# Softmax denominators from 32x32 transposes and one product, one more buffer for high parts, and a different order on VectorE and GpSimd in the second of two attention layers

## Chip, cores and metric

One core of one Trainium2 chip. The metric is the device time of one execution in microseconds (us), lower is better. Engines: TensorE (PE, with its weight loads shown apart as PEld), VectorE (DVE), ScalarE (ACT), GpSimd (POOL), and SyncE (SP), which only issues DMAs. SBUF is the on-chip memory, PSUM the small memory that TensorE writes to.

## The reference

Two self-attention layers over 4 images of 64x64 = 4096 tokens with 256 channels, float32:

```
# layer 0: q, k of width 32, v of width 256
q, k, v = x @ Wq + bq, x @ Wk + bk, x @ Wv + bv
x = gamma * softmax(q @ k.T) @ v + x
# layer 1: f (keys), g (queries) of width 32, v of width 128
f, g, v = x @ Wf + bf, x @ Wg + bg, x @ Wh + bh
x = x + (softmax(g @ f.T) @ v) @ Wo + bo
```

## The kernel before

`fast_path` holds the whole calculation (`general_path` runs only if a range test at the end finds values too large or too small; it did not run here). No maximum is subtracted: the kernel computes `p = exp(score)`, accumulates `p @ v`, and divides by the sum of p at the end.

**Tiling.** A `Step` is one score tile `st` of 128 keys x 1024 (four key tiles by 256 queries in layer 0, two key tiles by 512 queries in layer 1). A block is one set of queries against all keys: 8 steps in layer 0 (16 blocks per image), 16 steps in layer 1 (8 blocks per image). So there are 32 blocks of layer 1 in all. The loop over `steps` (L735) runs image by image, layer 0 then layer 1.

**What a step does.** `scores` (L523) puts the products k*q into PSUM and ScalarE takes `high` (a rounded exp, for split steps) and `p` (L542, L544). `cut_low` (L552) makes `low = p - high` on VectorE, `cut_both` (L557) makes `d` from low and high. TensorE then multiplies high, low and d with three forms of v, each in one pass of float32r. All layer 0 steps are split. In layer 1 only steps 0, 3, 5, 8, 11, 13 (`SPLIT1`) are; the other ten multiply `p` itself in full float32 (two instructions per product). Scores run two steps ahead of the products, and low one step ahead.

**Sums of p in layer 1.** For steps in `MOVED_SUMS` the sum is made by DMAs that GpSimd issues (L548 a copy for the first, L550 adding DMAs for the others) into the tile `p_sum_moved`. For the others VectorE adds into `p_sum` (`add_up`, L564). At the end of a block `end_second` (L654) adds the two (L659), folds 1024 columns to 512 (`sums`, L660), and returns four units, `output(t)`, one for each 128 queries. A unit multiplies the accumulated rows by Wo (L667) and, to get each query's denominator onto its own partition, multiplies the 128x128 block of `sums` by a column of ones (L668). VectorE inverts that column (L670), ScalarE scales the result (L673), GpSimd's queue adds it to `out` in memory by a DMA (L675).

**Order.** `plan` (L702) hands units to steps: the four output units of a block go to steps 1 to 4 of the next block. Projections of coming keys and values (`project_units`: transpose, qk, v) are dealt out in the same way over both layers. The framework traces instructions in program order, then orders each engine's queue itself by a model of readiness, so an engine's queue may differ from the program's order. Tiles with one `tag` share a ring of `bufs` buffers, and a new tile waits until the oldest user is done. The rings here: `t` (high parts, and p of split layer-1 steps) 2, `p` 3, `l` 2, `d` 1 (also p_sum), `e` 1 (p_sum_moved), `small` 4 (residual rows `x_res`, new rows `x1`, outputs `y`), `sums` 1, `qk` 1, `squares` 2; in PSUM `side` 2.

**End.** After the last unit, the range test (L807 to L822) runs over all inverses and decides by a flag whether the general path is needed.

Of the kernel before, what the change touches and what calls it, by code (L numbers as in the profile page):

```python
# [61 lines left out]
S = 32  # L62
# [5 lines left out]
SPLIT1 = (0, 3, 5, 8, 11, 13)  # L68
MOVED_SUMS = (0, 4, 7, 9, 12)

# [168 lines left out]
def fast_path(ctx: ExitStack, tc: tile.TileContext, x, w0, w1, wo, bo, gamma, out, off):  # L239
# [27 lines left out]
    def wide(tag, name, dtype=F32):  # L267
        return work.tile([P, 2 * QB], dtype, tag=tag, bufs={"d": 1, "e": 1, "p": 3}.get(tag, 2), name=name)

# [39 lines left out]
    nc.vector.memset(ones, 1.0)  # L309

    inverse = const.tile([P, 2, B * N // P], F32, name="inverse")
    seen_v = const.tile([P, 2, B * NH], F32, name="seen_v")
# [11 lines left out]
    for l, (q_w, q_b, k_w, k_b, v_w, v_b) in enumerate((w0, w1)):  # L324
        queue = (nc.scalar, nc.gpsimd)[l]
        w_sb = work.tile([P, NCC, 2 * D], F32, tag="small", bufs=4, name=f"wqk_whole{l}")
        b_sb = const.tile([2 * D, 1], F32, name=f"bqk{l}")
        for g, w_dram, b_dram in ((0, q_w, q_b), (D, k_w, k_b)):
            queue.dma_start(w_sb[:, :, g : g + D], w_dram.rearrange("(c p) d -> p c d", p=P))
            queue.dma_start(b_sb[g : g + D, :], b_dram.rearrange("(d o) -> d o", o=1))  # L330
        w_parts = const.tile([P, NCC, 4 * D], F32R, name=f"wqk{l}")
        high, low = w_parts[:, :, : 2 * D], w_parts[:, :, 2 * D :]
        nc.scalar.copy(high, w_sb)
        nc.vector.tensor_sub(low, w_sb, high.bitcast(F32))
        wqk.append(w_parts)
        bqk.append(b_sb)
        v_sb = const.tile([P, NCC, CV[l]], F32, name=f"wv{l}")
        queue.dma_start(v_sb, v_w.rearrange("(c p) d -> p c d", p=P))
        wv.append(v_sb)
# [20 lines left out]
    def bias_units():  # L360


        def issue():
            nc.vector.tensor_scalar(bv, bv, gamma_sb, None, ALU.mult)
            wide_bias = work.tile([P, P], F32, tag="small", bufs=4, name="wide_bias")
            nc.vector.memset(wide_bias, 1.0)
            nc.vector.tensor_scalar(wide_bias, wide_bias, bv1, None, ALU.mult)
            ps = side_psum("ps_bias")[:, :C]
            nc.tensor.matmul(ps, wide_bias, wo_sb, start=True, stop=True)
            nc.vector.tensor_add(bo_sb, bo_sb, ps)  # L370

        return [issue]

    xT, x_parts, k_t, v_t, halves = {}, {}, {}, {}, {}
    qk_dram, x1_dram = {}, {}
    q_t, moved_sums, first_p, waiting = {}, {}, [], {}

# [34 lines left out]
    def project_units(b, l, h):  # L412
# [5 lines left out]
        def qk_unit():  # L418
            ps = side_psum(f"psqk_{b}_{l}_{h}")[:, :QB0]
            for c in range(NCC):  # L420
                for n in range(2):
# [6 lines left out]
                    )  # L428
            whole = data.tile([2 * D, QB0], F32, tag="qk", name=f"qk_{b}_{l}_{h}")
            lead = b == l == 0 and h % 2 == 1  # L430
# [7 lines left out]
            top, bottom = slice(0, 2 * D), slice(2 * D, P)  # L438
            nc.scalar.copy(whole, ps[bottom, :])
            nc.vector.scalar_tensor_tensor(whole, ps[top, :], bqk[l], whole, ALU.add, ALU.add)  # L440
            nc.scalar.copy(parts[top, :], whole)
# [49 lines left out]
    def load_rows(dst, parts, which, order):  # L491
        for n, h in enumerate(order):
            nc.gpsimd.dma_start(dst[n * D : (n + 1) * D, :], parts[h, which])

# [15 lines left out]
    def small(name):  # L510
        return work.tile([P, C], F32, tag="small", bufs=4, name=name)


    class Step:
# [8 lines left out]
        def scores(self):  # L523
            b, l, j, i = self.b, self.l, self.j, self.i
            n = 2 * QB // G[l]
            q0 = j * n % QB
            index = j * NI[1] + i
            tag = "pair" if l == 1 and index > 0 and index % 2 == 0 else "st"
            st = ps_main.tile([P, G[l], n], F32, tag=tag, name=f"st_{self.key}")
            for g in range(G[l]):  # L530
                kt = G[l] * i + g
                nc.tensor.matmul(  # L532
                    st[:, g, :],
                    k_t[b, l, kt // NT][:, kt % NT * P : (kt % NT + 1) * P],
                    q_t[b, l, j * n // QB][:, q0 : q0 + n],
                    start=True,
                    stop=True,
                )
            s_flat = st.rearrange("p g n -> p (g n)")
            if self.split:  # L540
                self.high = wide("t", f"high_{self.key}", F32R)
                nc.scalar.activation(self.high, s_flat, AF.Exp, bias=down)  # L542
            self.p = wide("t" if self.split and l == 1 else "p", f"p_{self.key}")
            nc.scalar.activation(self.p, s_flat, AF.Exp)  # L544
            if l == 1 and i in MOVED_SUMS:
                if i == MOVED_SUMS[0]:
                    moved_sums[b, j] = wide("e", f"p_sum_moved_{b}_{j}")
                    nc.gpsimd.dma_start(moved_sums[b, j], self.p)  # L548
                else:
                    nc.gpsimd.dma_start(moved_sums[b, j], self.p, accum_op=ALU.add)  # L550

        def cut_low(self):  # L552
            if self.split:
                self.low = wide("l", f"low_{self.key}", F32R)
                nc.vector.tensor_sub(self.low, self.p, self.high.bitcast(F32))  # L555

        def cut_both(self):  # L557
            if self.split:
                self.d = wide("d" if self.l == 0 else "l", f"d_{self.key}", F32R)
                nc.vector.scalar_tensor_tensor(  # L560
                    self.d, self.low.bitcast(F32), -UP, self.high.bitcast(F32), ALU.mult, ALU.add
                )

        def add_up(self, p_sum):  # L564
            if self.l == 0 or self.i in MOVED_SUMS:
                return
            kept = [i for i in range(NI[1]) if i not in MOVED_SUMS]
            if self.i == kept[0]:
                first_p.append(self.p)
            elif self.i == kept[1]:  # L570
                nc.vector.tensor_add(p_sum, first_p.pop(0), self.p)
            else:
                nc.vector.tensor_add(p_sum, p_sum, self.p)  # L573

# [78 lines left out]

    def end_second(b, j, acc, p_sum, o):  # L654
        key = f"{b}_{j}"
        for h in range(QB // QB0):
            nc.vector.tensor_add(o[h][:, :QB0], o[h][:, :QB0], acc[1][:, h * QB0 : (h + 1) * QB0])
        sums = work.tile([P, QB], F32, tag="sums", bufs=1, name=f"sums_{key}")
        nc.vector.tensor_add(p_sum, p_sum, moved_sums[b, j])  # L659
        nc.vector.tensor_add(sums, p_sum[:, :QB], p_sum[:, QB:])  # L660

        def output(t):
            def issue():
# [3 lines left out]
                nc.tensor.matmul(ps[:, :C], part, wo_sb, start=True, stop=True)  # L667
                nc.tensor.matmul(ps[:, C : C + 1], sums[:, tok], ones[:, :1], start=True, stop=True)  # L668
                n = (b * N + j * QB) // P + t
                nc.vector.reciprocal(inverse[:, 1, n : n + 1], ps[:, C : C + 1])  # L670

# [6 lines left out]

        return [output(t) for t in range(NT)]

    def run(units):
        for u in units:
            u()


# [9 lines left out]
    steps[1].scores()  # L695
    steps[0].cut_low()
    beyond = Step(B, 1, 0, 0)
    beyond.scores, beyond.split = nothing, False
    keys = [(b, l, j) for b in range(B) for l in range(2) for j in range(NB)][NB:]
    acc, p_sum, units = None, None, {}  # L700

    def plan(b, l, j, ends):  # L702
# [20 lines left out]
        else:  # L723
            for n, u in enumerate(ends):
                put(1 + n, u)
        if b + 1 < B:
            for h in range(NH):
# [7 lines left out]
    for n, s in enumerate(steps):  # L735
        b, l, j = s.b, s.l, s.j
        if s.first:
            units = plan(b, l, j, ends)
            acc = [ps_main.tile([P, QB], F32, tag=f"acc{a}", name=f"acc{a}_{b}_{l}_{j}") for a in range(2)]
            if l == 0:  # L740
                pair = ps_main.tile([P, 2, QB], F32, tag="pair", name=f"acc_pair_{b}_{j}")
                acc += [pair[:, a, :] for a in range(2)]
            if l == 1:
                p_sum = wide("d", f"p_sum_{b}_{j}")
        if l == 0 and s.last:
# [20 lines left out]

        s.cut_both()
        after.cut_low()
        s.add_up(p_sum)
        todo = units.get(s.i, [])  # L770
# [30 lines left out]
        if s.last:  # L801
            ends = end_first(b, j, acc) if l == 0 else end_second(b, j, acc, p_sum, o)
    run(ends)

    good = small("good").rearrange("p (l n) -> p l n", l=2)  # L807
    nc.vector.tensor_scalar(good, inverse, 1.0 / SUM_MAX, None, ALU.is_ge)
    nc.vector.tensor_scalar(inverse, inverse, 1.0 / SUM_MIN, None, ALU.is_le)
    nc.vector.tensor_mul(good, good, inverse)  # L810
    nc.vector.tensor_scalar(seen_v, seen_v, VALUE_MAX, None, ALU.is_le)
    size = const.tile([P, 1], F32, name="size")
    nc.vector.tensor_mul(size, gamma_sb, gamma_sb)
    nc.vector.tensor_scalar(size, size, GAMMA_MAX**2, None, ALU.is_le)
    low = const.tile([P, 1], F32, name="low")
    for seen, axes in ((good, AX.XY), (seen_v, AX.XY)):
        nc.vector.tensor_reduce(low, seen, axes, ALU.min)
        nc.vector.tensor_mul(size, size, low)
    nc.vector.tensor_scalar(low, size, 1.0, None, ALU.is_lt)
# [53 lines left out]
```

## Time and profile before

| | us |
|---|---|
| median of 3 runs | 3158.69 (3158.46 to 3160.62) |
| the profiled execution's own time | 3155.92 |
| its span, first to last instruction | 3154.1 |
| TensorE matmul busy | 3116.3 (99%) |
| TensorE weight loads busy | 2672.0 (85%) |
| VectorE busy | 2689.1 (85%) |
| ScalarE busy | 2140.1 (68%) |
| GpSimd busy | 900.7 (29%) |
| granted TensorE clock | 0.998 of full |

Everything below is read from one profiled execution. Its own time is 2.8 us under the median of the unprofiled runs and 1.8 us over its span. "Busy" of TensorE is modelled: its matmuls are pipelined, so what counts is when the next one starts. A few per cent of matmul records can be missing from a trace.

### The profile page before, as it was taken

What the parts mean: (1) busy time and instruction counts of PE and PEld (TensorE: products, weight loads), DVE (VectorE), ACT (ScalarE), POOL (GpSimd) and SP (SyncE); (2) the same over time, 40 slices, a digit from 0 to 9 for tenths busy, and PEclk for the clock granted to TensorE, in tenths of its full rate; (3) what the DMA queues carried; (4) which work ended last, traced back from release to release, by engine and by line L of the source; (5) the groups of instructions that cost most, each with busy time, mean ns of one, the idle gap of its engine ahead of it and who ended that gap; (6) DMA issues with size and microseconds to landing.
All of it is one profiled execution on the core that took longest, in us unless ns stands there. A gap on an engine that the chain in (4) does not pass through costs nothing.

```text
span 3154.1 us, 54090 instructions
## 1 busy us (share of the span) xinstructions
PE 3116.3 (99%) x19908; PEld 2672.0 (85%) x19908; DVE 2689.1 (85%) x3237; ACT 2140.1 (68%) x2835; POOL 900.7 (29%) x1108
## 2 busy tenths in 40 slices
PE   8999999999999999999999999999999999999997
PEld 7999998666799999866679999976668999996664
DVE  7888888888888888888888888898888888888876
ACT  7666666777666666777766666677776666666674
POOL 5232224222422222422242222232223222233221
PEclk9999999999999999999999999999999999999999
DMA  4121114555512121555541112255554111125454
GB/s 119 43 53 47 48 48 104 107 108 105 104 44 51 41 53 47 113 101 112 107 93 47 49 45 51 51 116 107 105 113 81 48 46 47 49 65 105 97 95 73
DMA packets 391392, 239.49 MB, mean 76 GB/s; under 512 B 266672, under 2 KB 355248, under 8 KB 391120
## 3 DMA queue, kind: packets, MB, share of 16 engines
q0 software_dynamic: 68160, 134.86, 22.0%
q1 hardware_dynamic: 322048, 100.76, 13.4%
q8 instruction: 161, 2.64, 0.4%
q14 instruction: 111, 0.91, 0.1%
q10 hardware_dynamic: 912, 0.33, 0.1%
HBM read 82.58 MB, written 67.11 MB: 47 GB/s over the span
## 4 chain that ended last, share of the span: by engine, by line
PE 91%; DVE 3%; DMA 2%; issue 2%; ACT 1%; POOL 0%; SPq 0%; DVEq 0%; ACTq 0%; POOLq 0%
PE acc L600 24%; PE acc L582 23%; PE acc_pair L582 23%; PE st L532 14%; PE psv L464 4%; PE psqk L422 2%; PE pso L667 2%; DVE d L560 1%; DVE low L555 1%; ACT p L544 1%; DVE p_sum L573 1%; DMA p_sum_moved<-p 0%; DMA squares<-in_x 0%; PE pso L668 0%; DMA squares<-x_dram 0%
## 5 line engine op out<-in xcount | busy, mean ns | idle before, releaser
L542 ACT ACTIVATE high<-st,down 128x1024 fp32r<-128x1024 f32 x704 | 786.5, 1117 | 703.2 <-PE st L532 362.8
L544 ACT ACTIVATE p<-st 128x1024 f32<-128x1024 f32 x1024 | 1042.5, 1021 | 166.3 <-PE st L532 143.8
L560 DVE SCALAR_TENSOR_TENSOR d<-low,high 128x1024 fp32r<-128x1024 f32 x704 | 871.0, 1237 | 227.0 <-PE acc_pair L582 223.7
L555 DVE TENSOR_TENSOR low<-p,high 128x1024 fp32r<-128x1024 f32 x704 | 936.6, 1330 | 142.6 <-ACT p L544 141.6
L532 PE MATMUL st<-q,k 128*128 128x256 f32 (+1 forms) x3072 | 706.3, 338 | 2.5 <-DMA k<-qk_parts 1.4
L600 PE MATMUL acc<-p,v 128*128 128x512 f32 x1280 | 611.0, 597 | 0.0
L532 PEld LDWEIGHTS st<-q,k 128*128 128x128 f32 x3072 | 470.0, 189 | 103.3 <-issue 40.6
L639 POOL TENSOR_TENSOR x_res<-x,bo 128x256 f32<-128x256 f32 x128 | 212.5, 1660 | 879.3 <-DVE x L628 879.2
L600 PEld LDWEIGHTS acc<-p,v 128*128 128x128 f32 x1280 | 233.1, 189 | 161.8 <-issue 143.4
L573 DVE TENSOR_TENSOR p_sum<-p_sum,p 128x1024 f32<-128x1024 f32 x288 | 352.6, 1224 | 9.4 <-ACT p L544 5.8
L582 PE MATMUL acc<-v0h,high 128*128 128x258 f32 x2048 | 341.6, 284 | 1.2 <-ACT high L542 1.2
L582 PE MATMUL acc<-v0d,d 128*128 128x258 f32 x2048 | 339.2, 287 | 2.6 <-DVE d L560 2.2
L582 PE MATMUL acc<-v0l,low 128*128 128x256 f32 (+1 forms) x2048 | 329.3, 283 | 0.6 <-DVE low L555 0.5
L582 PE MATMUL acc_pair<-v0h,high 128*128 128x258 f32 x2048 | 329.8, 283 | 0.0
L582 PE MATMUL acc_pair<-v0l,low 128*128 128x256 f32 (+1 forms) x2048 | 328.8, 282 | 0.0
L582 PE MATMUL acc_pair<-v0d,d 128*128 128x258 f32 x2048 | 328.5, 282 | 0.0
L582 PEld LDWEIGHTS acc<-v0h,high 128*128 128x128 f32 x2048 | 286.0, 189 | 3.1 <-issue 1.4
L582 PEld LDWEIGHTS acc<-v0d,d 128*128 128x128 f32 x2048 | 281.5, 190 | 5.6 <-DVE d L560 4.9
L582 PEld LDWEIGHTS acc<-v0l,low 128*128 128x128 f32 x2048 | 282.2, 190 | 1.8 <-DVE low L555 1.3
L582 PEld LDWEIGHTS acc_pair<-v0h,high 128*128 128x128 f32 x2048 | 282.1, 189 | 0.0
L582 PEld LDWEIGHTS acc_pair<-v0l,low 128*128 128x128 f32 x2048 | 281.1, 189 | 0.0
L582 PEld LDWEIGHTS acc_pair<-v0d,d 128*128 128x128 f32 x2048 | 281.0, 189 | 0.0
(108 smaller groups left out, 3332.5 us busy)
## 6 DMA issues: line engine op xcount, KB each, us to landing
p_sum_moved<-p POOLq DMA_DIRECT2D x160, 512.0 KB, 4.7
x_res<-in_x SPq DMA_DIRECT2D x128, 128.0 KB, 2.1
qk_dram<-qk_parts SPq DMA_DIRECT2D x128, 128.0 KB, 1.9
x_dram<-x SPq DMA_DIRECT2D x128, 128.0 KB, 1.7
out<-x_res SPq DMA_DIRECT2D x128, 128.0 KB, 1.7
squares<-x_dram SPq DMA_DIRECT2D x512, 32.0 KB, 1.9
out<-y POOLq DMA_DIRECT2D x128, 128.0 KB, 3.2
q<-qk_dram POOLq DMA_DIRECT2D x252, 64.0 KB, 2.2
```

The source lines that it names most:

```text
L422: nc.tensor.matmul(ps, wqk[l][:, c, :], x_parts[key][n][:, c, :], start=(c == n == 0), stop=(c == NCC - 1 and n == 1),)
L464: nc.tensor.matmul(ps[:, t, :], xT[key][:, c, t * P : (t + 1) * P], wv[l][:, c, :], start=(c == 0), stop=(c == NCC - 1),)
L532: nc.tensor.matmul(st[:, g, :], k_t[b, l, kt // NT][:, kt % NT * P : (kt % NT + 1) * P], q_t[b, l, j * n // QB][:, q0 : q0 + n], start=Tru ...
L542: nc.scalar.activation(self.high, s_flat, AF.Exp, bias=down)
L544: nc.scalar.activation(self.p, s_flat, AF.Exp)
L555: nc.vector.tensor_sub(self.low, self.p, self.high.bitcast(F32))
L560: nc.vector.scalar_tensor_tensor(self.d, self.low.bitcast(F32), -UP, self.high.bitcast(F32), ALU.mult, ALU.add)
L573: nc.vector.tensor_add(p_sum, p_sum, self.p)
L582: nc.tensor.matmul(acc[2 * s + which][:, :width], p[:, g * QB0 + s * P : g * QB0 + (s + 1) * P], v0[self.i][v][:, g, :width], start=self.f ...
L600: nc.tensor.matmul(acc[which], v_part[:, g, :], p[:, g * QB : (g + 1) * QB], start=first and g == 0, stop=last and g == G[1] - 1,)
L639: nc.gpsimd.tensor_add(x_old[s], x_new[s], bo_sb)
L667: nc.tensor.matmul(ps[:, :C], part, wo_sb, start=True, stop=True)
```

## The change

In the second layer the six moved steps become (3, 4, 6, 7, 9, 12): the base is step 3's own p tile, written by ScalarE into ring `e`, so no copying DMA; five adding DMAs follow. VectorE's adds go from ten to nine in a block. The column of ones is replaced, in 31 of the 32 blocks, by two VectorE instructions (`turn`: a 32x32 block transpose of `sums`, and a sum over groups of 32 columns into `part_sums`, 128x16) and one product with a fixed 0/1 matrix `same` (`denominators`), followed by four inversions of 32 partitions x 4. These two units take steps 1 and 2 of the next block, the four output units steps 3 to 6. The last block keeps the column of ones. `sums` now lives in `p_sum`, in ring `d`, until `turn` has read it. `same` is built by GpSimd at the start with seven small instructions. Ring `t` has three buffers, `small` three, `sums` and `qk` are gone (the qk unit works in PSUM and in `qk_parts`). `issue_after` queues instructions of one engine behind a given one: in layer 1 what VectorE does after the cuts (sums, units) goes behind the latest low or d, and each adding DMA goes behind the last load of q or k traced before it. The range test is divided: all but the last block's inverses are tested in step 13 of the last block, the last four columns at the end.

```diff
-MOVED_SUMS = (0, 4, 7, 9, 12)
+MOVED_SUMS = (3, 4, 6, 7, 9, 12)
...
-        return work.tile([P, 2 * QB], dtype, tag=tag, bufs={"d": 1, "e": 1, "p": 3}.get(tag, 2), name=name)
+        return work.tile([P, 2 * QB], dtype, tag=tag, bufs={"d": 1, "e": 1, "p": 3, "t": 3}.get(tag, 2), name=name)
...
+    same = const.tile([P, P], F32, name="same")
+    nc.gpsimd.tensor_copy(same[:, :S], ident[:, :S])
+    for a in range(1, P // S):
+        nc.gpsimd.tensor_add(same[:, :S], same[:, :S], ident[:, a * S : (a + 1) * S])
+    for a in range(1, P // S):
+        nc.gpsimd.tensor_copy(same[:, a * S : (a + 1) * S], same[:, :S])
...
-            nc.scalar.copy(whole, ps[bottom, :])
-            nc.vector.scalar_tensor_tensor(whole, ps[top, :], bqk[l], whole, ALU.add, ALU.add)
+            whole, rest = ps[top, :], parts[top, :].bitcast(F32)
+            nc.scalar.copy(rest, ps[bottom, :])
+            nc.vector.scalar_tensor_tensor(whole, whole, bqk[l], rest, ALU.add, ALU.add)
...
-            nc.gpsimd.dma_start(dst[n * D : (n + 1) * D, :], parts[h, which])
+            loads[0] = nc.gpsimd.dma_start(dst[n * D : (n + 1) * D, :], parts[h, which])
...
-        return work.tile([P, C], F32, tag="small", bufs=4, name=name)
+        return work.tile([P, C], F32, tag="small", bufs=3, name=name)
...
+            base = l == 1 and i == MOVED_SUMS[0]
+            self.p = wide("e" if base else "t" if self.split and l == 1 else "p", f"p_{self.key}")
             nc.scalar.activation(self.p, s_flat, AF.Exp)
-            if l == 1 and i in MOVED_SUMS:
-                if i == MOVED_SUMS[0]:
-                    moved_sums[b, j] = wide("e", f"p_sum_moved_{b}_{j}")
-                    nc.gpsimd.dma_start(moved_sums[b, j], self.p)
-                else:
+            if base:
+                moved_sums[b, j] = self.p
+            elif l == 1 and i in MOVED_SUMS:
+                with tc.issue_after(loads[0].ins):
                     nc.gpsimd.dma_start(moved_sums[b, j], self.p, accum_op=ALU.add)
...
-        sums = work.tile([P, QB], F32, tag="sums", bufs=1, name=f"sums_{key}")
-        nc.vector.tensor_add(p_sum, p_sum, moved_sums[b, j])
-        nc.vector.tensor_add(sums, p_sum[:, :QB], p_sum[:, QB:])
+        sums, squares = p_sum[:, :QB], p_sum[:, QB:]
+        nc.vector.tensor_add(sums, sums, squares)
...
+        def turn():
+            nc.vector.transpose(squares, sums)
+            nc.vector.tensor_reduce(part_sums, squares.rearrange("p (n k) -> p n k", k=S), AX.X, ALU.add)
+        def denominators():
+            ps = side_psum(f"psd_{key}")[:, : QB // S]
+            nc.tensor.matmul(ps, same, part_sums, start=True, stop=True)
+            for a in range(P // S):
+                rows = slice(a * S, (a + 1) * S)
+                of_rows = ps[rows, :].rearrange("p (t a) -> p t a", a=P // S)[:, :, a]
+                nc.vector.reciprocal(inverse[rows, 1, n0 : n0 + NT], of_rows)
...
-                nc.tensor.matmul(ps[:, C : C + 1], sums[:, tok], ones[:, :1], start=True, stop=True)
-                nc.vector.reciprocal(inverse[:, 1, n : n + 1], ps[:, C : C + 1])
+                if end:
+                    nc.tensor.matmul(ps[:, C : C + 1], sums[:, tok], ones[:, :1], start=True, stop=True)
+                    nc.vector.reciprocal(inverse[:, 1, n : n + 1], ps[:, C : C + 1])
...
+        return ([] if end else [turn, denominators]) + [output(t) for t in range(NT)]
...
+        if (b, j) == (B - 1, NQ[1] - 1):
+            put(NI[1] - 3, check_all_but_last)
...
+        cuts = [s.cut_both(), after.cut_low()]
+        cut = next((c for c in reversed(cuts) if c is not None), cut)
+        behind_cuts = ExitStack()
+        if l == 1:
+            behind_cuts.enter_context(tc.issue_after(cut.ins))
```

## Prediction

> **What bounds the kernel now.** I read the page from the top: busy shares, then the chain that ended last, then the groups, then the chain in order of time inside one block.
>
> ```profile
> PE 3116.3 (99%) x19908; PEld 2672.0 (85%) x19908; DVE 2689.1 (85%) x3237; ACT 2140.1 (68%) x2835; POOL 900.7 (29%) x1108
> PE 91%; DVE 3%; DMA 2%; issue 2%; ACT 1%; POOL 0%; SPq 0%; DVEq 0%; ACTq 0%; POOLq 0%
> ```
>
> TensorE is the chain for 91% of the span. As its busy time is modelled, I check it by step lengths: the chain inside the first part of a layer-1 block (start, length, what).
>
> ```profile
> 2887.73 0.46 PE st L532 x2
> 2888.19 0.43 PE pso L667 x2
> 2888.62 0.12 PE pso L668 x2
> 2888.74 2.30 PE acc L600 x6
> 2891.03 0.46 PE st L532 x2
> ...
> 2900.58 0.45 PE st L532 x2
> 2901.03 2.18 PE acc L600 x6
> 2903.21 0.47 PE st L532 x2
> ```
>
> The reader is to see two equal steps, one with an output unit and one without. They take 2891.03 - 2887.73 = 3.30 and 2903.21 - 2900.58 = 2.63 us: a unit costs TensorE 0.67. Of that 0.43 is the product with Wo; the other 0.24 is the column of ones, 0.12 in its own row and 0.12 in what follows it (2.30 against 2.18). No wait stands between the pieces. Three blocks of the last image, in the view by windows, say the same: 35.51 us each, TensorE busy in all of it, VectorE in 28.4.
>
> ```profile
> 2959.02:2994.53 35.51, 35.51 (x125) 22.75 (x124) 28.36 (x31) 24.35 (x28) 9.55 (x14) 1.00 0.50 96
> 2994.53:3030.04 35.51, 35.51 (x125) 22.75 (x125) 28.37 (x31) 24.30 (x28) 9.57 (x14) 1.00 0.52 97
> ```
>
> So time falls where TensorE's queue loses work, and grows where something new makes it wait. The waits of the other engines are long but mostly not the bound:
>
> ```profile
> DVE d L560 <- PE acc_pair L582: 223.7, 282, 1.5
> ACT high L542 <- DVE low L555: 141.9, 102, 1.8
> ACT high L542 <- PE acc_pair L582: 110.3, 60, 2.3
> POOL p_sum_moved L550 <- DMA p_sum_moved<-p: 45.2, 13, 4.5
> ```
>
> The second and third are high parts waiting for a buffer of ring t; ScalarE can afford them (68% busy).
>
> **What the skill says.** (1) "Perfetto Trace Analysis", Identifying the Most-Contended Engine: matmul busy share is no measure of headroom. The step lengths above replace it. (2) "TensorE: Matmul & The Clock Gate", LDWEIGHTS: a weight load takes its columns over 1.2 per ns, so 107 ns for 128 columns by estimate. That is close to the two times 0.12 above: a one-column float32 product is two instructions, each with a load of 128 columns that has nothing to hide behind. (3) "VectorE: DVE Perf Modes", perf-mode tier table: tensor_reduce runs at one element a cycle. The trace agrees: 420 ns for 256 columns and 286 for 128 (L817), 1.05 ns a column. (4) The TensorE page, Architectural detail, calls VectorE's queue strictly first-in first-out; so a late instruction there holds up the cuts behind it. No row of this trace contradicts that.
>
> **The change part by part.**
>
> Denominators on TensorE. In 31 blocks four column products go, 4 x 0.24, and one product with `same` comes. It has the same two weight loads, 0.24, and 16 columns instead of one: a float32 pass of 512 columns takes 0.43 (1.72 for four), so 16 columns in two passes add 0.03. Net 31 x (0.96 - 0.27) = **-21.4 us**. This lies wholly on the path. Bounds: if part of the second 0.12 belongs to the Wo product, half, -10.7; the unit's total of 0.67 less 0.43 for Wo leaves no room for more.
>
> Denominators on VectorE, per block: out go one add of 1.22 (ten to nine) and four inversions of 0.16; in come a transpose of 128x512, 0.70 (L392), a sum over 128x512, 0.69 by the slope above, and four inversions of 32x4, taken as 0.16 each. Net +0.2 of a block of 35 to 41 us: nothing, covered by the 7 us that VectorE idles in a block of the last image (35.5 - 28.4), about 5 in the earlier images. What counts is order: `turn` must come before the new p_sum and before the next d of ring d, and the product before the four units. In the block at 2959, sums end at 2959.22, d ends 1.1 later, `turn` 1.4 after that: 2.5. TensorE reaches step 2's unit at 2962.52, about 0.67 earlier with one unit gone: 2.6 after sums. The product is just in time. In blocks with a projection's transpose in front (0.70) it may be some 0.6 late unless the framework queues it later. I take 0, bounds 0 and 0.35 a block (10.8).
>
> Image boundaries (3). The first d of the next image's layer 0 shares ring d with p_sum, which is now held until `turn` has read it: 1.4 us later. At 846.6 sums end there, d runs 847.65 to 848.87, TensorE uses it at 849.11, with two output units put before it as filler. Taken as 0.5 each, +1.5; bounds 0 and 1.2 each (3.6).
>
> Second-layer order, third t buffer. TensorE's own waits on low and d add up to about 4 us in all (2.2, 1.1 and smaller rows); I take **-1.0**, bounds 0 and -4. Ring t relieves ScalarE, hidden under TensorE: 0.
>
> Moved sums. 32 copies (0.55 of GpSimd's queue each) go. Step 3's p in ring e waits for the previous block's L659, which ran 2885.3 to 2886.5, before step 3's exp is due: 0. The five adding DMAs follow one another at 4.7 us each, 23.5 from about 6 us into the block (p of step 4), so the last lands near 30 of 35 us, or 4.7 after step 12's p at 24. Hidden with some 5 us to spare; without it L659, the sums and the units would be late. While one waits in GpSimd's queue for the one before it, or for the loads it now follows, the output DMAs, q and k loads behind it wait too; y keeps a `small` buffer meanwhile, and ScalarE would stand if it needed a fourth. The loads' own waits are for scores of earlier steps, so they end before the adding DMA's p is there: 0, with a bound of +3.
>
> Ring small, four to three: layer 0 uses two residual and two new tiles per block. In the block at 990 the first new tile's readers end at 992.16, the second is written at 993.16: a buffer is free 1.0 earlier. 0; the loss is a rival below. The qk unit in PSUM has the same four instructions: 0.
>
> Start: seven small GpSimd instructions, by the nearest rows (0.20 and 0.32 for 128x128) 1.4 to 2.2 us, before weight and bias loads; the queue idles 4.2 before the first key load, but VectorE waited 0.7 for gamma. +1.0, bounds 0 and 3.
>
> End: the final test shrinks to four columns and no longer waits 1.99 for an output DMA's buffer: -3.0. But the test of the rest, ten instructions of 0.15 to 0.43, 2.5 us, goes into VectorE's last steps, where it is busy from 3127.3 to 3135.8 without a break. 0, bounds -3 and +2.6.
>
> **Sum:** -21.4 + 1.5 - 1.0 + 1.0 = -19.9. Against the profiled execution's 3155.9 (span 3154.1): 3136.0. The runs' median is 2.8 above it, 3158.7, so the forecast is **3138.8**. With the small bounds it lies in 3131 to 3147. A measurement of this kernel can tell about 0.2%, 6 us, from no change.
>
> **Rivals.**
> A. Half the gain: TensorE waits 0.35 a block for part_sums, or only half of the 0.24 is the column's. For it: the margin of 0.1 above. Against it: VectorE's idle time, and a queue ordered by readiness. 3149.6.
> B. No gain: the change doesn't do what it says, as the framework puts `denominators` where TensorE waits 0.69 a block, or the weight load hides anyway. Against it: the step lengths. 3158.7.
> C. Slower: in layer 0 the early load of the next residual rows takes the first free `small` buffer and the second new tile must wait for the output DMA's landing. Place: VectorE, step 2 of each of 64 blocks; in the block at 990 from 993.16 to 993.94, 0.78. Behind it stand d and low, and TensorE waits for d. There d ended at 994.78 and was used at 995.61, so 0.83 of slack would just cover it; with none, 64 x 0.78 = +50, 3189. It decides from 0.31 a block (20 / 64). With 0.55 lost a block, 3174.
>
> **Chances.** Forecast 0.72, A 0.11, B 0.05, C 0.12. Faster by over 0.2% 0.83, within 0.2% 0.05, slower 0.12. The range, 3131 to 3156, holds the forecast and A, leaving out C and most of B.
>
> **What would show it.** Right: only 8 instructions left of the column of ones (4 units x 2), 62 of the product with `same`, blocks of 34.8 us in the last image with TensorE busy throughout, output units of 0.43 there, a transpose of 0.70 and a reduce near 0.69 31 times more. Wrong: a TensorE wait on part_sums or on ring d's release in each block, or waits of VectorE before the new residual rows; in layer 0, steps longer than now. If the last image's blocks stay at 35.5, the forecast is wrong at its first step.

## The result and the profile after

The changed kernel took **3197.88 us** (median of four runs, 3197.07 to 3198.99) beside 3158.57 for the kernel before: ratio 1.0126, interval 1.0112 to 1.0141. It is slower by 39 us; 3138.8 was forecast. The profiled execution has a span of 3197.1 us, against 3154.1.

The page's busy line says little: TensorE has 186 instructions less and nearly the same busy time (3119.0 us against 3116.3). (The page's chain breaks off early here, so its shares are no use; the chain inside a window is.)

```profile
PE 3119.0 (98%) x19722; PEld 2652.8 (83%) x19722; DVE 2693.3 (84%) x3272; ACT 2133.5 (67%) x2835; POOL 881.4 (28%) x1115
```

The chain at the start of a middle block of the last image (start, length, what), the place that answers to the lines shown of before:

```profile
2996.03 0.93 PE acc L611 x4
2996.95 0.47 PE st L540 x2
2997.43 0.02 issue
2997.45 1.13 ACT high L550
2998.58 0.04 issue
2998.62 3.53 PE acc L611 x9
3002.15 0.15 PE psd L685 x2
3002.30 0.95 PE acc L611 x2
3003.26 0.46 PE st L540 x2
3003.71 0.43 PE pso L696 x2
3004.14 0.70 PE acc L611 x3
```

The reader is to see two things. The output unit is 0.43 with nothing behind it, and `psd` 0.15: what the forecast promised for TensorE is there. And a step of ScalarE, 1.13, now lies in TensorE's chain. The block as a whole, in the view by windows (length, then the engines' busy time):

```profile
2990.57:3026.46 35.89, 35.15 (x119) 21.86 (x118) 29.08 (x33) 24.24 (x29) 9.90 (x14) 1.00 0.53 95
```

35.89 against 35.51, with 0.74 us in which TensorE isn't busy; the forecast had 34.8. Of the waits shown of before, d's for `acc_pair` is still there (engine, line, what it waited for: us, times, longest):

```profile
DVE d L570 <- PE acc_pair L593: 236.2, 278, 1.5
```

The two of ScalarE's high parts for ring t, 141.9 and 110.3 us, are no longer in the list, and in e12, which goes back to two buffers, such rows stand again (197.8 and 69.0). But ScalarE isn't less idle: before its high parts it stands 708 us in all, 703 before. TensorE's own waits have grown: of the rows below, those for high of L611, for `qk_dram` and for the qk unit's sum were not in the list of before at all, and st's for ScalarE's p was 0.8 us.

```profile
PE psqk L430 <- ACT xh L413: 11.0, 7, 3.0
PE st L540 <- ACT p L554: 9.5, 13, 1.5
PE acc L611 <- ACT high L550: 7.4, 10, 0.7
...
PE st L540 <- DMA k<-qk_dram: 3.2, 1, 3.2
PE pso L696 <- DVE o L670: 2.7, 1, 2.7
...
PE psqk L430 <- DVE qk_parts L450: 2.3, 4, 0.7
```

Taken stage by stage from the starts of the score products, the 43 us of span lie here: first scores -1.8 (20.5 against 22.3 us); layer 0 of the first image +7.3, of the others +4.5, +4.7, +3.9; layer 1 of the four images +5.6, +3.8, +5.1, +7.1; tail +2.9. In layer 1 the first block of an image is the worst: 43.6, 43.5, 43.5, 40.2 us against 38.6, 38.5, 38.6, 37.2; the second is 1.7 to 2.7 longer. The six blocks behind them in each of the first three images are mostly shorter than before, by 0.2 to 1.2, so there the change does gain; the block above, of the last image, is not typical of them. In layer 0 the first block behind the start is longer, and the first two behind each image boundary; most of the others agree within 0.1, a few differ by up to 0.8 in either direction.

The granted clock has a part in this. Near the end of each image's first layer-1 block TensorE waits 3.0 to 3.2 us for the last projections or keys, and beside each of these waits the clock granted to it is half of full for 3.4 us. For the first image, the wait in a window from 552 to 566, then a window of the stretch (the granted clock is the third number from the end):

```profile
PE psqk L430 <- ACT xh L413: 3.0, 1, 3.0
```

```profile
561.70:565.10 3.40, 3.40 (x11) 2.85 (x10) 0.48 (x1) 0.37 (x1) 0.00 (x0) 0.50 0.74 135
```

The trace of before has neither between its start and its tail. As an estimate, a stretch costs half of its length, so the four cost 7 of the 43 us. One trace supports this: of the layer-1 blocks of e13 only the third image's have such a stretch (6.8 us long), and the first two of them take 83.7 us against 80.4 in the second image.

### The profile page after: what moved, and what is told of

Same layout as the page of the kernel before. It is cut to its first block, busy times and chain, and to the rows that moved or that the text cites. A ratio compares the mean times of both kernels' runs of the same rounds, so it can differ in the third digit from the quotient of the medians.

```text
span 3197.1 us, 53469 instructions
## 1 busy us (share of the span) xinstructions
PE 3119.0 (98%) x19722; PEld 2652.8 (83%) x19722; DVE 2693.3 (84%) x3272; ACT 2133.5 (67%) x2835; POOL 881.4 (28%) x1115
## 5 line engine op out<-in xcount | busy, mean ns | idle before, releaser
L611 PE MATMUL acc<-p,v 128*128 128x512 f32 x1280 | 609.8, 594 | 0.0
L650 POOL TENSOR_TENSOR x_res<-x,bo 128x256 f32<-128x256 f32 x128 | 204.0, 1594 | 858.2 <-DVE x L639 858.0
L611 PEld LDWEIGHTS acc<-p,v 128*128 128x128 f32 x1280 | 237.7, 189 | 162.0 <-issue 135.7
L560 POOL DMA_DIRECT2D p<-p x160 | 142.1, 888 | 705.9 <-issue 192.4
L584 DVE TENSOR_TENSOR p_sum<-p_sum,p 128x1024 f32<-128x1024 f32 x256 | 312.0, 1219 | 10.9 <-ACT p L554 8.2
L593 PEld LDWEIGHTS acc<-v0d,d 128*128 128x128 f32 x2048 | 282.6, 190 | 12.8 <-DVE d L570 11.2
```

The source lines that it names most:

```text
L584: nc.vector.tensor_add(p_sums[self.b, self.j], so_far, self.p)
L593: nc.tensor.matmul(acc[2 * s + which][:, :width], p[:, g * QB0 + s * P : g * QB0 + (s + 1) * P], v0[self.i][v][:, g, :width], start=self.f ...
L611: nc.tensor.matmul(acc[which], v_part[:, g, :], p[:, g * QB : (g + 1) * QB], start=first and g == 0, stop=last and g == G[1] - 1,)
L650: nc.gpsimd.tensor_add(x_old[s], x_new[s], bo_sb)
```

## The experiments

The median of before differs a little between sets of runs (3156.2 to 3159.7), so each result is also given as a difference to the runs of before that it shared, and two experiments are compared by these differences. Below, "the rule" is the two lines that put what a layer-1 step issues on VectorE behind the latest low or d; "the qk unit" is the projection to queries and keys, whose sum the change keeps in PSUM. Block lengths are from one profiled execution each.

**e1, the rule taken out of the changed kernel.**

```diff
-        if l == 1:
-            behind_cuts.enter_context(tc.issue_after(cut.ins))
```

> The changed kernel without the rule that in layer 1 VectorE's other work queues behind the latest low or d. Order theory: the rule pushes the last add of p, the moved-sums add and the two adds that empty the second accumulator behind low and d of the next block, and TensorE waits about 1.1 us at 25 or so block starts and 3 us in each first block of layer 1; without it 3160 to 3170 (27 to 38 below the changed kernel's 3197.9). GpSimd theory (adding DMAs behind loads) and buffer theory (ring small of three): no change from this, 3194 to 3199. Denominator theory (holding p_sum for the turn is what makes TensorE wait): 3190 to 3199.

3168.74 us, ratio 1.0029 (1.0019 to 1.0039), +9.2. The rule costs 30 of the 39 us. What it does in the last image's middle blocks is seen in VectorE's timeline at a block's start (start, length, engine, line, operation). With the rule, block start 2990.57:

```profile
2990.53 2.55 DVE L584 TENSOR_TENSOR p_sum<-p_sum,p 128x1024 f32<-128x1024 f32 x2
2993.39 1.22 DVE L565 TENSOR_TENSOR low<-p,high 128x1024 fp32r<-128x1024 f32 x1 [0.31 <-PE acc L611]
2994.53 1.22 DVE L584 TENSOR_TENSOR p_sum<-p_sum,p 128x1024 f32<-128x1024 f32 x1
2995.66 1.22 DVE L570 SCALAR_TENSOR_TENSOR d<-low,high 128x1024 fp32r<-128x1024 f32 x1
2996.80 1.22 DVE L668 TENSOR_TENSOR p_sum<-p_sum,p 128x1024 f32<-128x1024 f32 x1
2998.05 0.75 DVE L670 TENSOR_TENSOR o<-o,acc 128x256 f32<-128x256 f32 x2
```

Without it, block start 2967.92:

```profile
2968.64 2.55 DVE L584 TENSOR_TENSOR p_sum<-p_sum,p 128x1024 f32<-128x1024 f32 x2
2971.10 1.22 DVE L565 TENSOR_TENSOR low<-p,high 128x1024 fp32r<-128x1024 f32 x1
2972.24 1.22 DVE L668 TENSOR_TENSOR p_sum<-p_sum,p 128x1024 f32<-128x1024 f32 x1
2973.49 0.75 DVE L670 TENSOR_TENSOR o<-o,acc 128x256 f32<-128x256 f32 x2
```

The last add of a block stands behind low, low waits 0.31 for its buffer, and d slips in before the block's end. L670 empties the second accumulator, which the next block's first whole product needs: it comes 7.5 us into the block in place of 5.6. In the chain shown above TensorE has another step's scores and high products there, and they wait for ScalarE (2996.95 to 2998.62).

**e2, the adding DMAs free of the loads** (`with tc.issue_after(loads[0].ins)` removed).

> The changed kernel with the adding DMAs no longer queued behind the loads of q and k. GpSimd theory: p's buffers come free earlier at the three image boundaries (ScalarE waited 1.4 us there for an adding DMA) and in the first blocks of layer 1: 10 to 15 less, 3183 to 3188. Order theory: 0 to 5 less, 3193 to 3198. Buffer and denominator theories: 3195 to 3199.

3198.37, ratio 1.0125 (1.0108 to 1.0142), +38.9: no effect. In the changed kernel GpSimd's new order is neither cost nor gain.

**e3, the denominators alone, put into the kernel before** (`same`, `turn`, `denominators`; `sums` keeps its own tile).

> The kernel before with the turn and the one product alone: moved sums, rings and orders as before, a tile of its own for sums, the turned copy written into the second half of p_sum. All theories that blame something else (order, GpSimd, buffers): the forecast's first term less small losses at the image boundaries, 3136 to 3143. Denominator theory: p_sum held until the turn, or the product waited for, eats the gain: 3152 to 3165, blocks of the last image at 35.2 us or more.

3159.19, ratio 1.0001 (0.9993 to 1.0010), -0.3: no gain. The last image's middle blocks:

```profile
2955.01:2990.44 35.43, 35.41 (x120) 21.85 (x118) 30.11 (x33) 24.10 (x29) 9.54 (x14) 1.00 0.51 97
```

TensorE's time in that block, summed by tile from the start of one product to the start of the next: scores 9.01 before, 9.31 here; accumulations 24.23 and 24.26; output units with `psd` 2.28 and 1.87. So the units give back 0.41 where 0.69 was priced, and the scores take 0.30 of that again. Of the 0.30, 0.17 is `psd` waiting for its sums (by this way of summing it falls to the score product ahead of it), and 0.11 a score product whose weight load waits until ScalarE has read its PSUM buffer for p (2971.95). TensorE's own list of waits has neither in this block. The list of its weight loads has both kinds over the whole run: 12.4 us for the sums of `psd` in 26 times, and 34.3 us of scores for p (23.4 before).

**e4, two buffers in ring t, four in ring small, in the changed kernel.**

> The changed kernel with ring t back at two buffers and ring small back at four. Buffer theory: the waits of x1 and y for output DMAs go (0.9 us each seen at the first blocks of layer 0, TensorE lost 1.1 to 1.5 there): 4 to 10 less, 3188 to 3194. Order, GpSimd and denominator theories: within 3 of 3197.9; if the third t buffer helped, more: 3199 to 3205.

3226.63, ratio 1.0216 (1.0199 to 1.0233), +67.1, 28 us above the changed kernel; TensorE's first wait is scores for ScalarE's p (20.0 us, 24 times). The third buffer in ring t doesn't hurt, it helps. As two rings changed at once, this run doesn't say what ring small costs; e16 does.

**e5, the block's end outside the rule** (`behind_cuts.close()` ahead of `end_second`).

> The changed kernel with one difference: the end of a layer-1 block (the adds of the moved sums, the two adds that empty the second accumulator, the add of the halves) is traced outside the rule that VectorE takes the low part first; the rest of the step stays under it. Theory 'block ends': nearly all of the rule's 29 us comes from the emptying of the second accumulator late, 1.06 us a block: the last image's middle blocks fall from 35.89 to about 35.1 and the time to 3166 to 3176. Rival 'all steps': the rule costs in every step (scores, projections, running adds behind the low part): the last image's blocks stay within 0.2 of 35.9 and the time is 3188 to 3198.

3192.57, ratio 1.0113 (1.0096 to 1.0130), +36.3: 3 us less, within what the intervals leave open. Middle blocks stay 35.88, with VectorE in the same order as in the changed kernel. The end isn't held by the rule but by the add it needs, which is.

**e6, the rule alone, in the kernel before.**

> The kernel before with only the rule that in the second layer what a step issues comes after its low part and d. Theory 'rule by itself': it costs here what it cost in the changed kernel, 29 us: 3180 to 3192, the last image's middle blocks 36.3 or more against 35.51, with a wait of the first products for the second accumulator. Rival 'rule only together': it costs only because the running add and d also changed places (other moved steps, third buffer): 3156 to 3165.

3218.67, ratio 1.0196 (1.0179 to 1.0213), **+62.4**: twice what it costs in the changed kernel, and outside both expectations. Ring t alone doesn't explain the double. In the changed kernel with two t buffers the rule costs about 33: e4's +67.1 less e12's +29.6 below and less the 4 that the qk unit's sum costs there (some more if e4's fourth small buffer helped). Stretches at half the clock come to 27 us in this trace (14 us of cost by the estimate above); the rest of the difference is open.

**e7, the query and key sum in PSUM alone, in the kernel before.**

> The kernel before with only the query and key sum kept in PSUM (no SBUF tile). Theory 'PSUM buffer held': the side buffer is held through all four instructions, so at the start TensorE's products wait about 0.7 each and the first layer-0 block is 5 to 7 us longer; nothing elsewhere: 3163 to 3166. If it also makes the first layer-1 block of each image longer (4 to 5 each), 3178 to 3186. Rival 'hidden', as the forecast had it: 3157 to 3161.

3166.42, ratio 1.0029 (1.0018 to 1.0040), +10.1. The first layer-0 block is 6.8 us longer. Two waits for the qk unit's last instruction that were not in the list of before:

```profile
PE psqk L422 <- DVE qk_parts L442: 2.0, 3, 0.7
...
PE psx L389 <- DVE qk_parts L442: 1.7, 2, 1.5
```

The third and fourth of the "same four instructions" now read PSUM too, so the side buffer is free later, and at the start nothing covers that.

**e8, e1 with that sum in SBUF in the first image's layer 0** (a tile of tag e, which is idle there).

> The changed kernel without the low-part rule, and with the query and key sum of the first image's layer 0 in SBUF again (in the buffer of tag e, unused then). Theory 'PSUM buffer held at the start': the first layer-0 block loses 5 to 6 us again: 3162 to 3165 against 3168.7 without the rule alone. Rival: the start is late for the product matrix on GpSimd and the changed loads: 3167 to 3170, first block within 1 us of the changed kernel's.

3161.40, ratio 1.0017 (1.0010 to 1.0024), +5.1: the first layer-0 block is back at 72.0 us (77.3 in e1). First layer-1 blocks are still 43.7, 41.8, 43.9, 40.9; the trace has a stretch at half the clock beside each of them but the second.

**e9, only the running add free of the rule.**

```diff
+        s.add_up()
         behind_cuts = ExitStack()
         if l == 1:
             behind_cuts.enter_context(tc.issue_after(cut.ins))
-        s.add_up()
```

> The changed kernel with one difference: the running add of a step (p into p_sum) is traced ahead of the rule, so that it need not come behind the low part; scores, projections and block ends stay under it. Theory 'running add held': at a block's start the add of the last p waits behind low, the block's end behind that add, and the emptying of the second accumulator comes 7.5 us into the block where it came 5.6; with the add free the last image's middle blocks fall from 35.89 to 35.1 to 35.3 and the time to 3165 to 3176. Rival 'scores held': the rule acts through the scores and high parts behind it: 3187 or more.

3176.70, ratio 1.0061 (1.0045 to 1.0078), +20.4. Middle blocks fall to 35.1. So 19 of the rule's 30 us come from the running add held behind low. The other 11 lie in what else of VectorE's work stands under the rule (its parts of the projections and of the output units, and the block's end); the scores, which have no VectorE instruction, can at most be held indirectly.

**e10, the list of moved sums alone, in the kernel before** (`MOVED_SUMS = (3, 4, 6, 7, 9, 12)`).

> The kernel before with only the list of moved sums changed (steps 3, 4, 6, 7, 9, 12 in place of 0, 4, 7, 9, 12; the copy is kept, at step 3). Theory 'early adds': the running adds now stand at steps 1, 2, 5 in place of 2, 3, 5, 6, beside the residual units of layer 1's first block; there the new rows and the turned loads come later, and each image's first layer-1 block is 3 to 5 us longer, the rest within 1 us: 3166 to 3178. Rival: the first block's loss comes from the ring small of three or the third t buffer: first blocks within 1 us of before, 3154 to 3161.

3196.88, ratio 1.0124 (1.0107 to 1.0141), **+40.6**, far more than either theory had. First layer-1 blocks are 46.2, 44.7, 44.8, 45.0, and TensorE's first wait is new keys:

```profile
PE st L532 <- DMA k<-qk_dram: 19.4, 4, 5.7
```

The scores at the end of that block need the layer's last keys, the end of a long chain: new rows of layer 0 (L628), their write to memory, the load back for the projection, transpose, projection, write, key load. With running adds at steps 1 and 2, the first new rows come 11.1 us into the block (7.5 before, 8.2 in the last image). The trace's stretches at half the clock, all in first blocks of a layer, come to 34 us: by the estimate above 17 of the 40.6.

**e11, e8 with the adds of steps 1 and 2 one step later.**

> The changed kernel without the low-part rule, with the query and key sum of the first image's layer 0 in SBUF, and with the running adds of layer-1 steps 1 and 2 traced one step later (2 and 3), where the kernel before had them. Theory 'early adds': each image's first layer-1 block comes back to 38 to 39.5 us (last image 36.5 to 37.5) from 42 to 44 (40.9), and the time is 3142 to 3150, faster than before (3156 to 3159). Rival: first blocks stay above 41: 3158 to 3164.

3157.34, ratio 1.0003 (0.9994 to 1.0012), +1.1. First blocks 41.3, 41.7, 41.6, 40.6, above 41 in three of four as the rival had it; the time lies between the two ranges. So early adds are a part only. The first new rows come at 8.0 us (7.5 before), the second 3.7 later (1.6 before), and their write, issued 0.7 behind an adding DMA of 512 KB, lands after 4.5 us in place of 1.8.

**e12, e8 with two buffers in ring t.**

> The changed kernel without the low-part rule, with the query and key sum of the first image's layer 0 in SBUF, and with two buffers in ring t. Theory 'third buffer carries the gain': without it ScalarE's high parts come late, and the last image's middle blocks go back from 35.1 to 35.4 or more: 3170 to 3185 against 3161. Rival 'hidden', as the forecast priced it: within 3 us of 3161, blocks 35.1.

3185.87, ratio 1.0088 (1.0071 to 1.0105), +29.6, 24.5 more than e8; the middle block shown here is 35.50 (35.1 in e8). By the estimate above, 5 of the 24.5 are longer stretches at half the clock (24 us here, 14 in e8).

```profile
2985.24:3020.74 35.50, 35.41 (x120) 21.74 (x118) 29.22 (x32) 23.55 (x29) 9.22 (x14) 1.00 0.54 95
```

**e13, e8 with the moved sums of before** (list and copy of the kernel before). Run with **e14**, the same with a product of a column of ones given back in each unit (its result isn't read):

```diff
+                if not end:
+                    nc.tensor.matmul(ps[:, C : C + 1], part, ones[:, :1], start=True, stop=True)
```

> The changed kernel without the low-part rule, with the query and key sum of the first image's layer 0 in SBUF, and with the moved sums of the kernel before (steps 0, 4, 7, 9, 12, the copy at step 0). What stays is the product for the denominators, three buffers in ring t, three in ring small, the reused p_sum. Theory 'moved sums own the first block': each image's first layer-1 block comes back to 38 to 39.5 us (last image 37 to 37.5), the last image's middle blocks stay at 35.0 to 35.2: 3139 to 3147, faster than before. Rival 'three buffers in small or ring d': first blocks stay above 41: 3157 to 3164.

> The same as e13, with a product of a column of ones added in each of the 124 output units outside the last block (its result isn't read; it costs TensorE the two instructions that the change removed). Theory 'with a third buffer TensorE's work counts': the last image's middle blocks grow by 0.7 to 1.0 us to 35.8 to 36.1, and the time is 20 to 30 us above e13. Rival 'hidden, as it was with two buffers': blocks grow by under 0.2 and the time by under 6 us.

e13: 3152.32, ratio 0.9985 (0.9977 to 0.9992), -3.9, between the two theories' ranges. e14: 3176.89, ratio 1.0068 (1.0054 to 1.0082), **24.6 above e13**. The block of e13, then of e14:

```profile
2954.27:2989.35 35.08, 35.08 (x120) 22.00 (x119) 30.02 (x33) 24.32 (x29) 9.54 (x14) 1.00 0.52 98
```

```profile
2970.49:3006.50 36.01, 36.01 (x127) 22.91 (x126) 30.05 (x33) 24.32 (x29) 9.54 (x14) 1.00 0.52 96
```

By tile: scores 9.15 and 9.15, accumulations 24.34 and 24.32, units 1.59 and 2.54. All of the 0.93 is in the units: with a third buffer TensorE's work counts in full. First blocks of e13: 39.3, 39.0, 41.1, 39.3, each 1.6 to 4.4 shorter than in e8. The new rows still stand 3.7 us apart.

**e15, e11 with one adding DMA held back in the first block.**

> As e11 (no low-part rule, query and key sum of the start in SBUF, adds of steps 1 and 2 one step later), and in the first layer-1 block of an image the adding DMA of step 4 is issued only with that of step 6. Theory 'adding DMA beside the new rows': the write of the second new rows to memory lands again 1.7 to 2.5 us after issue in place of 4.5, the turned rows come 3 us earlier, and each image's first layer-1 block falls from 41.3 to 38.5 to 40 (last image 40.6 to 37 to 39): 3147 to 3154 against 3157. Rival 'not the DMA': first blocks stay within 0.7 of 41.3: 3155 to 3160.

3158.22, ratio 1.0005 (0.9998 to 1.0012), +2.0: first blocks 41.0, 40.2, 40.8, 40.5. The edit missed its aim: the first adding DMA was still issued 11.6 us into the block and landed at 16.7. So it says nothing on the collision.

**e16, e13 with layer 0's new rows written over o.**

```diff
-                x_new[s] = small(f"x1_{key}_{s}")
+                x_new[s] = o[s][:, :C]
```

> As e13, and the new rows of layer 0 are written over the output rows o they come from, not into a buffer of ring small. Theory 'ring small of three': in the first layer-1 block the second new rows come 1.6 us after the first again (3.7 in e13, where a buffer came free only when the output write of the first had landed), and each image's first layer-1 block falls from 39.0 to 41.1 (last 39.3) to 38.3 to 39 (last 36.7 to 37.5); the second layer-0 block behind an image's boundary gives its 1.4 us back: 3143 to 3149 against 3152. Rival: VectorE's order alone sets it: spacing still 3.5 or more, 3150 to 3155.

**3144.56, ratio 0.9958 (0.9944 to 0.9972): faster than both kernels**, by 15.1 than before. The two new rows stand together, at 7.0 and 7.4 us into the block, in one line of VectorE's timeline; in e13 the second came behind low and an add:

```profile
2838.87 0.88 DVE L642 SCALAR_TENSOR_TENSOR o<-o,g,x_res 128x256 f32<-128x256 f32 x2
```

First blocks are 38.5, 38.5, 38.5, 38.2, and no stretch at half the clock stands beside them. The second layer-0 block behind a boundary stays about 0.9 above before (1.4 in e8), so that part of the expectation held in part.

## Why the prediction was wrong, step by step

The forecast failed in terms that it put at or near nothing. Taken out one after the other, they lead from the changed kernel's +39.3 to +9.2 (the rule, e1), +5.1 (the qk unit's sum, e8), -3.9 (the moved sums, e13) and -15.1 (ring small, e16). So the rule costs 30.1, the sum 4.1, the list 9.0 and the ring 11.2, each in this order of taking out. What is left of the change gains 15.1, where its sum was -19.9.

- **"Second-layer order, third t buffer", -1.0 (0 to -4): the step that failed most.** The rule was priced by the waits of TensorE that it might remove, and not by what it puts behind low. It costs 30 us here (e1) and 62 in the kernel before (e6); 19 of the 30 are the running add (e9). The third buffer was priced at 0, as relieving only an engine with time to spare. It is worth 24.5 us (e12 against e8). ScalarE's idle share of 32% was no help where it counts: with two buffers its high part starts only when an older one has been read, which are the 141.9 and 110.3 us that the prediction showed.
- **"Moved sums", 0 (+3).** It looked at the adding DMAs and not at where the remaining adds went. The list alone costs 40.6 us in the kernel before (e10); putting the old one back gains 9.0 in e13 against e8. In the two traces the first layer-1 blocks are 11.5 us shorter in sum, and part of that is given back elsewhere.
- **"Denominators on TensorE", -21.4.** The price was right and its condition missing. e14 gives the columns back: 0.93 in the block shown, where 4 x 0.24 was priced, and 24.6 us in all, where 31 x 0.96 makes 29.8. (A weight load of the column's product is listed at 189 ns in the trace of before, not near the 107 by estimate; the 0.24 rests on the step lengths, which held.) But in the kernel before, the same product gains nothing (e3), since the scores take up what the units leave. "No wait stands between the pieces" doesn't say how far off the next wait is.
- **"Denominators on VectorE", 0.** Durations held: transpose 0.71, sum 0.68, inversions 0.18 each for 0.16. "Just in time" held too: 0.17 of waiting in e3, within the bound of 0.35.
- **"Image boundaries", +1.5.** The denominators alone cost 0.6 at each first block of layer 0, near the 0.5 priced, but 0.8 more at the second: 4.3 in all, over the bound of 3.6 (e3). In the changed kernel the first blocks are longer by 2.7, 2.7 and 2.3 us, and that is the rule: in e1 they are 0.3 shorter than before, the second ones still 1.3 to 1.7 longer.
- **"Ring small", 0.** Rival C had the mechanism and the wrong place: not in 64 layer-0 blocks, most of whose lengths are unchanged, but in the first layer-1 block, where the second new rows come late and the last keys hang on them, and in the second layer-0 block behind a boundary. Taking the new rows out of the ring gains 11.2 (e16 against e13).
- **"The qk unit in PSUM", 0.** It counted instructions and not how long the PSUM buffer is held: +10.1 alone (e7), about 4 in the changed kernel (e8 against e1).
- **"Start", +1.0.** No cost of the GpSimd instructions is seen: in the runs that have them the first scores come from 1.8 us earlier to 0.9 later than before. The first block's loss is the qk unit's. **"End", 0 (to +2.6):** the tail is 2.9 longer, just over the bound. The last output units wait 2.7 for L670, and ten instructions of the range test stand among VectorE's last adds before it (3171.11 to 3176.24); no run takes them out.

Rival B's time of no gain was close for e3, for a reason near its own: TensorE waits, but in several places, little in each.

Still open: why the list of moved sums and the rule each cost more in the kernel before (e10, e6) than in the changed one, also beside the clock's part; what the late landing of the new rows' write costs the kernel (e15 did not remove it); and which of VectorE's work carries the last 11 us of the rule. No run holds the clock at full, so its share is an estimate. And no run puts only the product and the third buffer into the kernel before: that the two gain together rests on e3, e12 and e14.

## What to carry to other kernels

Before a saving on the busiest engine is counted, ask how late its next operand is: a chain without gaps may be just met by two other engines, and here it took one buffer more to make the saving real. Price an ordering rule by everything that it puts behind its anchor, down to the instruction that frees an accumulator. An edit that "costs nothing" in the steady state is to be followed through the first block of each stage, where one long chain of writes and loads has no cover; a wait of a few us there can also bring a stretch at a lower clock.

## What was not expected of the hardware

The writes of new rows, 128 KB each, landed 1.7 us after their issue in the median. In the changed kernel, e1, e8 and e11 one write per image was issued 2.6, 1.6, 1.6 and 0.7 us behind an adding DMA of 512 KB, on another queue; it took 2.3, 3.4, 3.4 and 4.5 us. In all these 16 cases it landed 0.2 to 0.4 us after that adding DMA. In all 18 traces together 53 writes were issued while an adding DMA was under way, and none landed before it. Why is not shown.

From 110 us to the last block, all 22 waits of TensorE of 3.0 us or more in these traces have a stretch at half the clock beside them, 3.4 or 6.8 us long. Of the waits of 1.8 to 2.9 us some have one and some don't (in e1 the 2.8 us that end at 562.4 have none, the 2.8 us that end at 1339.0 have one). The four traces without a wait of 1.8 us or more there (before, e3, e7, e16) have no such stretch there.

TensorE was 99% busy by the page in the kernel before, and yet of the 0.69 us that was to be taken from its work in a block only 0.08 came off the block (35.43 in e3) with two buffers in ring t. In e13, with three and with the rest of what it keeps of the change, it was 0.43 (35.08).
